# Folding two normalisation factors into one gate factor: k and v of a linear-attention layer are no longer scaled one by one

## The chip, the cores and the metric

The kernel runs on one core of a Trainium2 chip. A core has five engines that run their own instruction streams and wait for each other through semaphores: TensorE (PE in the profile, with its weight loads as PEld) for matrix products, VectorE (DVE) and GpSimd (POOL) for elementwise work on 128 partitions, ScalarE (ACT) for activation functions and copies, and SyncE (SP), which here starts transfers. The metric is the device time of one execution in microseconds (us).

## The reference, cut to what matters

The program is a network of four layers on a 256-channel image of 64 x 64 points, so on 4096 tokens of 256 features. Layers 0 and 1 are convolution-like; layer 2 is a gated linear attention and a mixture of experts; layer 3 is a softmax attention and another mixture of experts. Only the attention of layer 2 is touched. Its core is this (8 heads, 32 features a head; `L` is the token axis):

```python
q, k, v = (linear(x, w) for each of the three)           # (B, H, L, 32)
sim = einsum('bhld,bhld->bhl', q, k) * qk_norm_scale      # from the raw k
k = k / max(|k|, 1e-12)                                   # length over the 32 features of a head
v = v / max(|v|, 1e-12)
Z = einsum('bhld,bhle->bhlde', v, k) * kv_norm_scale
gates = square(relu(<Z, wg_w> + wg_b)) + 1e-5             # one number for each token and head
Z_scan = cumsum(gates * Z)                                # along the tokens
g_scan = cumsum(gates)
w = softmax-like weight from a running maximum and sum of sim
ctxt = q . (Z_scan / (g_scan + 1e-5)) * (1 + silu(w))
out = linear(ctxt, wo)
```

Everything that uses the normalised k and v uses their product Z. So the two lengths enter only as one factor r = 1/(|k||v|) for each token and head.

## The kernel before: the parts that matter

The 4096 tokens are 32 tiles of 128 (`NT`), worked on in 8 blocks (`NBLK`) of 4 tiles (`TPB`) with 512 tokens (`NB`). Inside the block the order of TensorE's instructions is the order of the calls below; the order on the other engines is chosen by a scheduler from the dependences.

```python
stages = [self.attn2_project(b, t, A, wg_bd, wp, ps) for b in range(NBLK)]
go = lambda b, *names: [stages[b][nm]() for nm in names if 0 <= b < NBLK]
with tc.manual_schedule(engines={mybir.EngineType.PE}):
    go(0, "norm", "turn")
    for b in range(-1, NBLK):
        go(b + 2, "norm")
        go(b + 1, 0)                # project tile 0 of the next block
        go(b, "lengths")
        go(b + 1, 1, 2)
        go(b, "sims")
        go(b + 1, 3)
        go(b, "turn_v")
        go(b + 2, "turn")
        go(b, "gates")
self.attn2_fac(A)                   # scans over all tokens: needs every gate and sim
```

The stages of a block (`attn2_project`, cut):

```python
room = lambda: wp.tile([P, TPB, C], F32, tag="room", name="a2_room", bufs=3)

def turn():                                                       # normalised tokens -> channels
    held["nT"] = wp.tile([P, 2, NB], F32, tag="nT", name="a2_nT", bufs=1)
    self.to_channels(ps, "a", held["n"], held["nT"], on_act=True)  # 8 PE transposes, 2 ACT copies

def project(i):
    ti, nT = b * TPB + i, held["nT"]
    for dst, lo, hi in ((A["qk"][:, ti, :], 0, 2 * C), (A["v"][:, ti, :], 2 * C, 3 * C)):
        p = ps.tile([P, hi - lo], F32, tag="b", name="a2_qkv_ps", bufs=4)
        self.mm(p, [(nT[:, kt, i * P : (i + 1) * P], w["w_qkv2"][:, kt, lo:hi]) for kt in range(2)])
        nc.vector.tensor_add(dst, p, self.row("b_qkv2")[:, lo:hi])                    # L1290

def lengths():
    ss = wp.tile([P, 2, TPB, NH], F32, tag="ss", name="a2_ss")
    for j, x in ((1, v), (0, k)):
        sq = room()
        nc.scalar.activation(sq, x, AF.Square)                                        # L1297
        nc.vector.tensor_reduce(ss[:, j], heads(sq), AX.X, ALU.add)                   # L1298
    held["tmp"] = room()
    nc.gpsimd.tensor_tensor(held["tmp"], q, k, ALU.mult)                              # L1300
    nc.vector.tensor_scalar_max(ss, ss, 1e-24)                                        # L1301
    nc.scalar.activation(ss, ss, AF.Sqrt)                                             # L1302
    nc.vector.reciprocal(ss, ss)                                                      # L1303
    nc.vector.tensor_mul(heads(v), heads(v), bc(ss[:, 1], 3, D))                      # L1304
    nc.gpsimd.tensor_tensor(heads(k), heads(k), bc(ss[:, 0], 3, D), ALU.mult)         # L1305

def sims():
    sim = wp.tile([P, TPB, NH], F32, tag="sim", name="a2_simt")
    nc.vector.tensor_reduce(sim, heads(held["tmp"]), AX.X, ALU.add)                   # L1309
    nc.vector.tensor_tensor(of("sim"), by_tile(sim), ..., ALU.mult)                   # L1310

def turn_v():
    self.to_channels(ps, "a", v, vT, on_act=True)        # 8 PE transposes, 2 ACT copies to a_vT (L226)

def gates():
    u = room()
    for i in range(0, TPB, 2):
        p = ps.tile([P, 2, 2, P], F32, tag="u", name="a2_u_ps")
        for j in range(2):
            for m in range(2):
                self.mm(p[:, j, m, :], [(vT[:, m, (i + j) * P : (i + j + 1) * P], wg_bd[:, m, :])])
        nc.vector.tensor_mul(u[:, i : i + 2, :], p..., k[:, i : i + 2, :])            # L1322
    g = wp.tile([P, TPB, NH], F32, tag="g", name="a2_g")
    nc.vector.tensor_reduce(g, heads(u), AX.X, ALU.add)                               # L1324
    nc.vector.tensor_scalar(g, g, self.row("wg_b"), 0.0, ALU.add, ALU.max)            # L1325
    nc.vector.tensor_mul(g, g, g)                                                     # L1326
    nc.vector.tensor_scalar_add(g, g, 1e-5)                                           # L1327
    nc.scalar.copy(of("gate"), by_tile(g))                                            # L1328
    nc.gpsimd.tensor_tensor(heads(k), heads(k), bc(g, 3, D), ALU.mult)                # L1329
```

The later stage (`attn2_sum`) reads v, vT and the gated k only in products of v with k.

Of the kernel before, what the change touches and what calls it, by code (L numbers as in the profile page):

```python
# [10 lines left out]
F32 = mybir.dt.float32  # L11
# [3 lines left out]
ALU = mybir.AluOpType  # L15
# [4 lines left out]
P = 128  # L20
# [6 lines left out]
TPB = NB // P  # L27
NH = 8
D = C // NH
# [51 lines left out]
def bc(ap, axis, n):  # L81

    ap = ap.unsqueeze(axis)
    shape = list(ap.shape)
    shape[axis] = n
    return ap.to_broadcast(shape)


class Net:
# [1088 lines left out]
    def attn2(self, t, S):  # L1178

        nc, tc = self.nc, self.tc  # L1180
        with tc.tile_pool(name="a2", bufs=1) as pool:
            A = {}
            A["qk"] = pool.tile([P, NT, 2 * C], F32, tag="qk", name="a2_qk")
            A["v"] = pool.tile([P, NT, C], F32, tag="v", name="a2_v")
            A["vT"] = pool.tile([P, 2, N], F32, tag="vT", name="a2_vT")

            for nm in ("sim", "gate", "fac"):
                A[nm] = pool.tile([P, 2, NT // 2, NH], F32, tag=nm, name=f"a2_{nm}")
            wg_bd = pool.tile([P, 2, P], F32, tag="wg_bd", name="wg_bd")
            self.kv_blocks(pool, None, wg_bd)  # L1190

            ked = pool.tile([P, 2, D], F32, tag="ked", name="a2_ked")
            nc.sync.dma_start(out=ked, in_=self.A["kvn_ed"].rearrange("(m p d) -> p m d", p=P, d=D))
            dif = pool.tile([P, 2, D], F32, tag="dif", name="a2_dif")
            nc.vector.tensor_tensor(dif, ked, bc(ked[:, :, 0], 2, D), ALU.not_equal)
            nc.vector.tensor_reduce(self.flags[:, 1:2], dif.rearrange("p m d -> p (m d)"), AX.X, ALU.max)
            with (
                tc.tile_pool(name="a2w", bufs=2) as wp,
                tc.tile_pool(name="a2_ps", bufs=2, space=PSUM) as ps,
            ):  # L1200
                self.rows(wp, "b_qkv2", "b_qkv2")
# [6 lines that stand above are left out]
                    for b in range(-1, NBLK):  # L1208
                        go(b + 2, "norm")
                        go(b + 1, 0)  # L1210
                        go(b, "lengths")
                        go(b + 1, 1, 2)
                        go(b, "sims")
                        go(b + 1, 3)
                        go(b, "turn_v")
                        go(b + 2, "turn")
                        go(b, "gates")
            self.attn2_fac(A)
            with (
                tc.tile_pool(name="a2x", bufs=2) as wp,  # L1220
                tc.tile_pool(name="a2x_ps", bufs=1, space=PSUM) as ps,
            ):
                bank = lambda: ps.tile([P, NB], F32, tag="r", name="f_r_ps")

                def route(t0, T):

                    n = A["qk"][:, t0 : t0 + T, :].rearrange("p t c -> p (t c)")[:, : T * CX]
                    nT = A["v"][:, t0 : t0 + T, :].rearrange("p t c -> p (t c)").rearrange("p (a n) -> p a n", a=2)
                    return self.route(t0, T, t, S, wp, n.rearrange("p (i c) -> p i c", c=CX), nT, bank)

                self.attn2_sum(t, A, ked, wp, ps, route)
            with (
                tc.tile_pool(name="a2t", bufs=1) as wp,
                tc.tile_pool(name="a2t_ps", bufs=1, space=PSUM) as ps,
            ):
                self.tile_table(S, wp, lambda: ps.tile([P, NB], F32, tag="r", name="f_r_ps"))
# [26 lines left out]

    def attn2_project(self, b, t, A, wg_bd, wp, ps):

        nc, w = self.nc, self.w
        tiles = slice(b * TPB, (b + 1) * TPB)
        pairs = slice(2 * b, 2 * b + 2)
        heads = lambda x: x.rearrange("p t (h d) -> p t h d", d=D)
        of = lambda nm: A[nm].rearrange("p a s h -> p s a h")[:, pairs]  # L1270
        by_tile = lambda x: x.rearrange("p (s a) h -> p s a h", a=2)
        q, k, v = A["qk"][:, tiles, 0:C], A["qk"][:, tiles, C:], A["v"][:, tiles, :]
        vT = A["vT"][:, :, b * NB : (b + 1) * NB]
        room = lambda: wp.tile([P, TPB, C], F32, tag="room", name="a2_room", bufs=3)
        held = {}

        def norm():
            held["n"] = wp.tile([P, TPB, C], F32, tag="n", name="a2_n", bufs=1)
            self.layer_norm(wp, t[:, tiles, :], held["n"], 1e-5, on_act=True)

        def turn():
            held["nT"] = wp.tile([P, 2, NB], F32, tag="nT", name="a2_nT", bufs=1)
            self.to_channels(ps, "a", held["n"], held["nT"], on_act=True)
# [16 lines that stand above are left out]
            nc.gpsimd.tensor_tensor(held["tmp"], q, k, ALU.mult)  # L1300
            nc.vector.tensor_scalar_max(ss, ss, 1e-24)  # L1301
            nc.scalar.activation(ss, ss, AF.Sqrt)  # L1302
            nc.vector.reciprocal(ss, ss)  # L1303
            nc.vector.tensor_mul(heads(v), heads(v), bc(ss[:, 1], 3, D))  # L1304
            nc.gpsimd.tensor_tensor(heads(k), heads(k), bc(ss[:, 0], 3, D), ALU.mult)  # L1305

        def sims():
            sim = wp.tile([P, TPB, NH], F32, tag="sim", name="a2_simt")
            nc.vector.tensor_reduce(sim, heads(held["tmp"]), AX.X, ALU.add)  # L1309
            nc.vector.tensor_tensor(of("sim"), by_tile(sim), bc(bc(self.row("qk_scale"), 1, 2), 1, 2), ALU.mult)  # L1310

        def turn_v():
            self.to_channels(ps, "a", v, vT, on_act=True)
# [8 lines that stand above are left out]
                nc.vector.tensor_mul(u[:, i : i + 2, :], p.rearrange("p t m c -> p t (m c)"), k[:, i : i + 2, :])  # L1322
            g = wp.tile([P, TPB, NH], F32, tag="g", name="a2_g")
            nc.vector.tensor_reduce(g, heads(u), AX.X, ALU.add)  # L1324
            nc.vector.tensor_scalar(g, g, self.row("wg_b"), 0.0, ALU.add, ALU.max)  # L1325
            nc.vector.tensor_mul(g, g, g)  # L1326
            nc.vector.tensor_scalar_add(g, g, 1e-5)  # L1327
            nc.scalar.copy(of("gate"), by_tile(g))  # L1328
            nc.gpsimd.tensor_tensor(heads(k), heads(k), bc(g, 3, D), ALU.mult)  # L1329

        call = lambda i: lambda: project(i)
        return {"norm": norm, "turn": turn, "lengths": lengths, "sims": sims, "turn_v": turn_v, "gates": gates,
                **{i: call(i) for i in range(TPB)}}

# [1297 lines left out]
```

## Time and profile before

The time before is 3652.96 us, the median of 3 runs (3647.47 to 3655.02). The profiled execution took 3723 us with the profiler on, a span of 3721.3 us. The table has the busy time of each engine over the whole span and over the steady part of the stage that the change touches. The stage reaches from the first projection of layer 2 (1635 us from the span's start) to the end of the last multiplication of k by its gate (1782.5 us): some 147 us or 4% of the span.

| engine | busy, whole span | share | busy, 1652 to 1780 us (128 us) |
|---|---|---|---|
| PE | 3365.0 us | 90% | 104.80 us |
| DVE | 2352.6 us | 63% | 114.30 us |
| ACT | 1413.8 us | 38% | 42.75 us |
| POOL | 1658.5 us | 45% | 58.87 us |

How to read it: the left columns say that the whole program is TensorE's; the right column says that this stage is not, at least not alone, since VectorE is the busiest engine there. No transfers of note run in the stage (1 GB/s). Lines of the profile name the engine, the source line (L1304 is the line with that comment above), the operation and the tile; "x8" is a count of instructions. TensorE's records come in pairs, two for each fp32 matrix product, and its transposes appear as `tr_ps`.

### The profile page before, as it was taken

To read this page: it belongs to the slowest core of one execution; us is meant where nothing else is said; L and a number is where in the kernel's file an instruction comes from. 1 tells how busy PE (TensorE), PEld (TensorE's weight loads), DVE (VectorE), ACT (ScalarE), POOL (GpSimd) and SP (SyncE) were. 2 spreads that over 40 slices of the span, in tenths; PEclk is the share of its full clock that TensorE was granted. 3 is DMA by queue.
4 is the path that set the end of the run, shared out by engine and by line. 5 is a ranking of instruction groups with operands and counts; after the bars stand their busy time and mean duration, and the time that the engine had idled before them with its cause. 6 is when DMAs were issued, how large, how long until landed. Compare 5 with 4: busy or idle time off the path is not lost.

```text
span 3721.3 us, 62677 instructions
## 1 busy us (share of the span) xinstructions
PE 3365.0 (90%) x23572; PEld 2388.9 (64%) x23572; DVE 2352.6 (63%) x5662; ACT 1413.8 (38%) x2891; POOL 1658.5 (45%) x1595
## 2 busy tenths in 40 slices
PE   6989999999997789888685887999999997999997
PEld 4443333333333688865564665788888886899886
DVE  6756656656565467779544547677777776555553
ACT  5544343343433566523232335322222222333332
POOL 1038888888885255634323344300000001555552
PEclk9999999999998899999786998999999998999999
DMA  1013404401012422210011865322233321555555
GB/s 57 3 28 107 137 26 124 138 24 41 21 34 94 123 63 71 72 33 1 13 36 58 261 215 217 135 90 93 95 98 97 97 91 52 219 204 209 198 192 190
DMA packets 160703, 377.44 MB, mean 101 GB/s; under 512 B 17345, under 2 KB 75458, under 8 KB 151170
## 3 DMA queue, kind: packets, MB, share of 16 engines
q1 hardware_dynamic: 136162, 317.91, 26.4%
q0 software_dynamic: 13056, 35.93, 2.5%
q10 hardware_dynamic: 11168, 19.42, 1.5%
q8 instruction: 192, 3.15, 0.4%
q14 instruction: 125, 1.02, 0.1%
HBM read 273.44 MB, written 99.76 MB: 100 GB/s over the span
## 4 chain that ended last, share of the span: by engine, by line
PE 39%; DVE 8%; issue 5%; DMA 5%; ACT 3%; POOL 3%; SPq 0%; POOLq 0%; DVEq 0%; ACTq 0%
PE a_sa_ps L2256 6%; PE f_h_ps L146 5%; PE a_oa_ps L2295 3%; PE a_ob_ps L2295 3%; PE a_oc_ps L2295 3%; DMA ys<-f_y,f_at 3%; PE a_sb_ps L2256 3%; PE f_ya_ps L146 2%; PE l_acc_ps L957 2%; PE f_yb_ps L146 2%; POOL ys L2010 1%; PE a_od_ps L2295 1%; PE a_q_ps L146 1%; PE a_sc_ps L2256 1%; PE a_s L1450 1%
## 5 line engine op out<-in xcount | busy, mean ns | idle before, releaser
L584 POOL TENSOR_TENSOR l_sm<-l_sc,mask 128x512 f32<-128x512 f32 (+3 forms) x624 | 770.7, 1272 | 119.2 <-ACT l_sc L574 116.8
L578 DVE TENSOR_TENSOR l_sm<-l_s,mask 128x256 f32<-128x256 f32 (+3 forms) x1248 | 492.3, 448 | 301.8 <-PE l_s L568 292.1
L574 ACT COPY l_sc<-l_s 128x384 f32<-128x384 f32 (+3 forms) x896 | 367.7, 461 | 558.5 <-PE l_s L568 533.5
L568 PE MATMUL l_s<-l_q,l_k 32*128 32x384 f32 (+2 forms) x3584 | 423.9, 513 | 7.4 <-ACT l_sc L574 4.1
L1826 POOL DMA_INDIRECT xs<-f_room,f_to x64 | 64.5, 1008 | 700.2 <-issue 587.2
L146 PE MATMUL f_h_ps<-f_xT,f_w 128*128 128x256 f32 x1440 | 343.2, 389 | 21.1 <-DVE f_xT L1930 8.5
L568 PEld LDWEIGHTS l_s<-l_q,l_k 32*128 32x128 f32 x3584 | 165.1, 183 | 240.7 <-issue 123.4
L146 PEld LDWEIGHTS f_h_ps<-f_xT,f_w 128*128 128x128 f32 x1440 | 262.0, 192 | 86.5 <-ACT f_h L1940 20.5
L2275 ACT ACTIVATE a_e<-a_e 128x512 f32<-128x512 f32 x256 | 155.9, 629 | 245.2 <-DVE a_e L2245 232.6
L1940 ACT ACTIVATE f_h<-f_h_ps,f_w 128x256 f32<-128x256 f32 x360 | 166.2, 470 | 169.9 <-PE f_h_ps L146 167.3
L953 DVE TENSOR_TENSOR l_pr<-l_vk,l_w_ps 128x1280 f32<-128x1280 f32 x128 | 186.6, 1482 | 54.5 <-PE l_acc_ps L957 36.2
L2010 POOL DMA_INDIRECT ys<-f_y,f_at x144 | 145.9, 1013 | 150.3 <-ACT f_y L2009 90.2
L957 PE MATMUL l_acc_ps<-ident,l_pr 128*128 128x128 f32 x1600 | 197.4, 277 | 8.2 <-POOL l_pr L948 8.1
L957 PEld LDWEIGHTS l_acc_ps<-ident,l_pr 128*128 128x128 f32 x1600 | 184.0, 143 | 14.9 <-POOL l_pr L948 9.9
L1967 POOL TENSOR_TENSOR f_wt<-f_w 128x512 f32<-128x512 f32 x72 | 90.0, 1271 | 211.5 <-PE f_ya_ps L146 198.1
L611 PE MATMUL l_a_ps<-l_sm,l_v 128*32 128x512 f32 (+3 forms) x1408 | 178.5, 528 | 2.5 <-POOL l_sm L584 2.4
L611 PE MATMUL l_b_ps<-l_sm,l_v 128*32 128x256 f32 (+2 forms) x2176 | 171.6, 376 | 0.5 <-POOL l_sm L584 0.5
L2256 PE MATMUL a_sa_ps<-a_q,a_kt 128*128 128x256 f32 x512 | 156.6, 388 | 12.7 <-DVE a_u L2261 11.6
L2260 ACT COPY a_u<-a_sa_ps 128x256 f32<-128x256 f32 x128 | 47.6, 372 | 293.6 <-PE a_sa_ps L2256 291.5
L2256 PE MATMUL a_sa_ps<-a_qt,a_kt 128*128 128x256 f32 x512 | 152.7, 380 | 0.0
L2256 PE MATMUL a_sb_ps<-a_qt,a_kt 128*128 128x256 f32 x512 | 131.4, 379 | 0.0
L2295 PE MATMUL a_ob_ps<-a_et,a_vs 128*128 128x256 f32 x512 | 131.4, 379 | 0.0
(532 smaller groups left out, 6942.1 us busy)
## 6 DMA issues: line engine op xcount, KB each, us to landing
a_kt<-a_kd SPq DMA_DIRECT2D x128, 512.0 KB
f_w<-in_f_w SPq DMA_DIRECT2D x36, 1152.0 KB
f_w<-in_f_w SPq DMA_DIRECT2D x36, 1028.0 KB
xs<-zero SPq DMA_DIRECT2D x8, 4160.0 KB
l_vk<-vt SPq DMA_DIRECT2D x180, 128.0 KB
f_x<-xs SPq DMA_DIRECT2D x72, 260.0 KB
f_w<-in_f_w SPq DMA_DIRECT2D x36, 384.0 KB
l_rcp<-l_recd SPq DMA_DIRECT2D x48, 256.0 KB
```

Of the source, the lines that this page charges most:

```text
L146: self.nc.tensor.matmul(out, lhsT, rhs, start=(i == 0), stop=(i == len(pairs) - 1))
L568: nc.tensor.matmul(s[pair, j], k[hp, key * P : (key + 1) * P], qs[hp], start=True, stop=True)
L574: nc.scalar.copy(sc[:, j], s[1, j])
L578: nc.vector.tensor_tensor(sms[0][:, j, at : at + t * wide].rearrange("p (t n) -> p t n", n=wide), part[:, which, :], mask, ALU.mult)
L584: nc.gpsimd.tensor_tensor(sms[1][:, :, at : at + t * wide].rearrange("p j (t n) -> p j t n", n=wide), part[:, :, which, :], bc(mask, 1, 2) ...
L611: nc.tensor.matmul(out, v[:, key, hp], sms[pair][:, j, base + lo * wide : base + hi * wide], start=not seen[nm], stop=(left[nm] == 0 and h ...
L953: nc.vector.tensor_tensor(pr, vk, bc(held["w"][:, j, dy], 3, D), ALU.mult)
L957: nc.tensor.matmul(acc[:, m, j, :], pf[:, dx, m * P : (m + 1) * P], self.ident, is_transpose=True, start=(j == 0 and dy == 0 and dx == 0 a ...
L1940: nc.scalar.activation(h[:, m, :], q, AF.Gelu, bias=w1[:, 2 * hidden + m : 2 * hidden + m + 1])
L2010: nc.gpsimd.indirect_dma_start(out=self.ys_parts[(i % 4) * NI + k], in_=y[:, k, :], in_offset=None, out_offset=bass.IndirectOffsetOnAxis(a ...
L2256: mm = lambda out, i, right: nc.tensor.matmul(out, A[i], right, start=True, stop=True)
L2295: nc.tensor.matmul(out, vs[:, j, i, :], right, start=(j == 0 and side != 1), stop=(j == NPAIR - 1 and side != 0))
```

## The change

Three things are changed. The factor r = 1/(|k||v|) is made once for a block (a product of the two lengths and a reciprocal of half the size), and neither v nor k is multiplied by its own factor any more: the pass over v on VectorE (L1304) and one pass over k on GpSimd (L1305) go. The gate's argument and, after the gate has been stored, the gate itself are each multiplied by r on 128 x 32 elements, so that the one remaining pass over k brings in gate and both lengths. And since v needs nothing but its projection now, its transposes move in TensorE's order from behind the next block's four projections to right behind the first of them. The purpose is to take work from the two elementwise engines and to free TensorE's transposes of v from a wait for VectorE.

```diff
@@ attn2
                         go(b + 2, "norm")
                         go(b + 1, 0)
-                        go(b, "lengths")
+                        go(b, "turn_v", "lengths")
                         go(b + 1, 1, 2)
                         go(b, "sims")
                         go(b + 1, 3)
-                        go(b, "turn_v")
                         go(b + 2, "turn")
                         go(b, "gates")
@@ attn2_project, lengths()
             nc.vector.tensor_scalar_max(ss, ss, 1e-24)
             nc.scalar.activation(ss, ss, AF.Sqrt)
-            nc.vector.reciprocal(ss, ss)
-            nc.vector.tensor_mul(heads(v), heads(v), bc(ss[:, 1], 3, D))
-            nc.gpsimd.tensor_tensor(heads(k), heads(k), bc(ss[:, 0], 3, D), ALU.mult)
+            held["r"] = wp.tile([P, TPB, NH], F32, tag="r", name="a2_r")
+            nc.vector.tensor_mul(held["r"], ss[:, 0], ss[:, 1])
+            nc.vector.reciprocal(held["r"], held["r"])
@@ attn2_project, gates()
             nc.vector.tensor_reduce(g, heads(u), AX.X, ALU.add)
+            nc.vector.tensor_mul(g, g, held["r"])
             nc.vector.tensor_scalar(g, g, self.row("wg_b"), 0.0, ALU.add, ALU.max)
             nc.vector.tensor_mul(g, g, g)
             nc.vector.tensor_scalar_add(g, g, 1e-5)
             nc.scalar.copy(of("gate"), by_tile(g))
+            nc.vector.tensor_mul(g, g, held["r"])
             nc.gpsimd.tensor_tensor(heads(k), heads(k), bc(g, 3, D), ALU.mult)
```

In the instruction streams, nothing outside this stage changes its place. Inside it, TensorE's stream differs only in the seven moved groups of transposes. The scheduler orders VectorE's steady block anew like this (t0 to t3 are the tiles of the projections that are under way): sum for sim, reciprocal of r, add of t2, `sim`, the layer norm's small steps, add of t3, the two products with u, sum for the gate, add of t0 for q and k, first gate times r, add of t0 for v, L1325's successor, the two sums of squares with the gate's steps between them, add of t1 for q and k, second gate times r, maximum of the squared lengths, add of t1 for v, product of the two lengths, and again the sum for sim.

## Prediction

> **What bounds the kernel now.** I read the windows first, since the page's shares cover 3721 us and the change touches 147 of them. Each window here runs from one block's transposes of v to the next's; the columns are length, busy time (and count) of PE, PEld, DVE, ACT, POOL, then the granted TensorE clock, the DMA share and GB/s.
>
> ```profile
> 1692.70:1709.45 16.75, 14.59 (x64) 9.37 (x65) 15.65 (x25) 6.58 (x13) 8.32 (x5) 1.00 0.00 0
> 1709.45:1726.05 16.60, 14.59 (x65) 9.37 (x65) 15.58 (x24) 6.49 (x12) 8.32 (x5) 1.00 0.00 1
> 1759.12:1771.77 12.65, 4.90 (x24) 4.21 (x25) 10.36 (x18) 3.55 (x6) 3.61 (x2) 0.70 0.00 1
> ```
>
> A steady block takes 16.6 us. DVE is busy for 15.6 of it, PE for 14.6, and no transfer runs. So DVE sets the pace, but only 2.0 us above PE. The third window is the tail behind the last projection, where PE is mostly idle.
>
> The chain of work that ended last shows the order inside a block (start, length, engine, tile, line):
>
> ```profile
> 1710.76 1.14 PE tr_ps L223 x8
> 1711.90 1.80 PE a_u_ps L146 x16
> ...
> 1716.27 1.87 DVE a_g L1325
> ...
> 1722.22 0.55 DVE a_ss L1303
> 1722.77 0.54 DVE a_qk L1290
> 1723.31 2.60 DVE a_v L1304
> 1725.91 0.14 issue
> 1726.05 0.64 PE tr_ps L223 x4
> ```
>
> It is a loop: PE's transposes of v wait for the scaling of v (L1304), the products with u come behind them, and everything from the gate's sum to L1304 is DVE again. The table of waits, taken over the stage, says how often:
>
> ```profile
> PE tr_ps L223 <- DVE a_v L1304: 17.6, 7, 7.5
> ```
>
> Seven waits, 17.6 us, the longest 7.5 us in the tail; the six others are (17.6 - 7.5) / 6 = 1.7 us each.
>
> Last the timeline of DVE and POOL, because L1304 takes 2.67 us in a steady block and 1.21 us at its fastest:
>
> ```profile
> 1722.91 1.91 POOL L1305 TENSOR_TENSOR a_qk<-a_qk,a_ss 128x1024 f32<-128x1024 f32 x1 [1.07 <-DVE a_ss L1303]
> 1723.23 2.67 DVE L1304 TENSOR_TENSOR a_v<-a_v,a_ss 128x1024 f32<-128x1024 f32 x1
> 1715.75 2.35 POOL L1300 TENSOR_TENSOR a_room<-a_qk 128x1024 f32<-128x1024 f32 x1
> 1716.18 1.95 DVE L1325 TENSOR_SCALAR a_g<-a_g,pr 128x32 f32<-128x32 f32 x1
> ```
>
> POOL's L1305 ends at 1724.82 and DVE's L1304 only 1.08 us later, about its own length: it stood still until POOL was through. L1325, on 32 elements, ends at 1718.13, just behind POOL's L1300 (1718.10); with POOL idle it took 0.24 us. So a block's DVE time holds waits for POOL: 1.46 us in L1304, some 1.65 in L1325, 0.3 in L1301.
>
> **What the Trainium skill says.** "SBUF — State Buffer", section "SBUF: two separate sides", calls the port pair that DVE and GpSimd share an exclusive lock: whoever starts first has it for the whole instruction, against a DVE operation in a 2-port mode or with two SBUF inputs. The lines above agree to 0.1 us. Its section "Who interferes with whom" adds that an operation with at most one SBUF input outside these modes doesn't contend; the reductions (1.20 us, under POOL or not) and the adds out of PSUM agree. By this the new products with r, two SBUF inputs each, can be caught as L1325 is now. "VectorE: DVE Perf Modes", section "The TRN2 errata — SBUF-src ops pay a fixed extra latency per instruction", gives (N+151)/0.96 ns for an fp32 tensor_tensor: estimates of 1224 ns for 1024 elements and 191 ns for 32. The trace has 1210 and 177 ns, and I use those. "TensorE: Matmul & The Clock Gate", section "Part 1: The HAM clock gate (the "warmup" mystery)", says an idle PE drops to half clock; the tail's 0.70 agrees.
>
> **The change, part by part.** I count DVE by steps, the distance from one start to the next, since instructions overlap by about 0.1 us.
>
> Removed from DVE in a block: the pass over v, 2.60 us, and the reciprocal of 64 elements, 0.47. Added: the reciprocal of 32 (0.55 us for 64 and 0.16 for 4 in the layer norm give 6.5 ns an element, 0.34 us, a step near 0.3) and three products of 32 elements at 0.18 us, steps of 0.1 to 0.2. POOL loses 1.91 us a block, and is no bound.
>
> The waits for POOL are what I can least read off the diff, so I walked the new order with the steps of 1709.57 to 1726.16:
> - sum for sim 1.12, reciprocal 0.3, add t2 0.93, sim 0.1, layer norm 0.4, add t3 0.93, two products with u 1.6, gate's sum 1.14, add t0 of q and k 0.6. Together 7.12.
> - First gate times r. L1300 starts as soon as the gate's sum has freed its buffer, 0.6 us earlier, and takes 2.35, so this product inherits L1325's wait: 1.85. L1325's successor then costs 0.2.
> - add t0 of v 0.33, two sums of squares with the gate's steps 2.44, add t1 of q and k 0.6, second gate times r 0.17, maximum 0.1, add t1 of v 0.4. With the line before, 13.2.
> - Product of the lengths. It starts some 0.6 us after the second gate product released POOL's pass over k (1.91 us), and has two SBUF inputs: about 1.45.
>
> The sum is 14.7 us, and 15.0 in the early blocks, which also have 0.37 us of layer-norm statistics. Of the 2.6 us of L1304, then, 1.1 was work and 1.5 was waiting, and the waiting partly comes back elsewhere.
>
> PE keeps its 14.6 us a block. Its transposes of v now come behind a projection (2.7 us), the transposes of n and the products with u, about 5.8 us after the end of the last tile's projection, while the add they need is due within 0.6 to 2.2 us. So the 1.64 and the 0.24 us waits of a block go. PE floor and DVE chain are equal within 0.4 us; I take 14.9 for the block, 1.7 less than now.
>
> Now the stage. Before, the projections of blocks 2 and 7 start at 1663.3 and 1746.7: five periods. Five at 14.9 save **9.0 us**. In the head, the first transposes of v go between earlier projections and the ACT copy between two groups falls out: **0.4 us**.
>
> The tail, from the last block's first projection: now 1746.7 to 1782.5, 35.8 us. After, PE needs 12.0 for four projections and a group of transposes, and the last v is in SBUF at about 13.8. From there DVE again: products with u of block 6 until 15.4, first sum of squares and gate's sum until 17.6, the other sum until 18.8, gate times r behind L1300 until 20.1, sum for sim until 21.3, small steps, products with u of block 7 and reciprocal until 23.7, gate's sum 24.9, gate times r behind POOL's pass of block 6 until 25.6, the gate's steps and its ACT copy until 26.7, POOL's last pass until 28.7. That is 28.8 against 35.8, **7.0 us**: the scaling of v no longer stands between the lengths and the transposes.
>
> In sum 9.0 + 0.4 + 7.0 = 16.4 us. The scans behind the stage need every gate, so what is saved here moves all that follows, and nothing else runs during the stage.
>
> **Rivals.** *All of L1304's 2.6 us leaves the loop.* If the new products slip in before POOL takes the port, DVE needs 14.7 less the 3.0 of waits and PE binds at 14.6: another 1.5 us over five blocks, and one or two in the tail; about 3634. For it: small operations often start ahead of POOL, as the tail's L1304 did (1.21 us, and POOL's L1305 stretched to 2.89). Against: L1325 is caught by L1300 in six of eight blocks.
>
> *A new wait takes the place of the old.* The second gate product also waits for ACT's copy of the gate, which stands behind the copies of vT in ACT's queue and so behind PE. The product of lengths waits for a square root on ACT. If the two add 1 us a block beyond my walk, DVE paces at some 15.9 us, and 3.5 us are left of the nine: about 3643. Against: an add of 0.4 to 0.6 us lies between each pair, ACT's small steps took 0.22 and 0.26 us, and PE has slack.
>
> *The saving disappears later.* A later stage waiting for a transfer would absorb it, leaving 3652. Against: the DMA share is 0.00 here, so no transfer spans the stage.
>
> **Range and chances.** 3652.96 - 16.4 = 3636.6, so 3637 us. The runs before spread by 7.5 us, so a median is good to some 3 us; the stage's saving I believe between 9 and 22 us. That gives 3629 to 3646. Two per cent are 73 us, half of the whole stage, so within 2% has 0.98, and either side 0.01.
>
> **What would show it.** Windows of about 14.9 us between transposes of v, with PE above 95% busy; the wait of `tr_ps` for L1304 replaced by next to nothing; the first product of gate and r near 1.9 us and the product of lengths above 1 us in the timeline, each ending with a POOL pass; the stage's end some 16 us earlier. It is wrong if periods stay above 15.5 us, if PE's transposes of v wait for the last add of v, or if the stage shortens and the end does not.

## The result, and the profile after

The changed kernel takes 3633.14 us, the median of 4 runs (3630.96 to 3635.90), against 3653.99 us before (4 runs, 3647.47 to 3655.97). That is 20.85 us less; the ratio is 0.9946, with a 95% interval from 0.9929 to 0.9964. The forecast was 3637 us, with 3629 to 3646.

The spans of profiles can't be compared across chips here: the kernel before took 3653 us on one chip and medians of 3719 to 3721 us on three others, a difference three times the size of the effect. The profiler is not the reason: the changed kernel's profiled execution took 3632.83 us, like its other runs. So times are compared only within one chip, and the profiles only by the stage. Its length, from the first projection of layer 2 to the end of the last multiplication of k by its gate, was 147.46 us (1635.04 to 1782.50) and is 125.82 us (1633.75 to 1759.57). The 21.6 us that the stage lost agree with the 20.85 us of the whole.

The windows of the changed kernel, from one block's transposes of v to the next's (columns as in the prediction: length, busy time and count of PE, PEld, DVE, ACT, POOL, clock, DMA share, GB/s):

```profile
1678.43:1693.22 14.79, 14.12 (x65) 9.44 (x64) 14.76 (x27) 6.58 (x14) 6.40 (x4) 1.00 0.00 0
1693.22:1708.02 14.80, 14.13 (x66) 9.44 (x65) 14.73 (x26) 6.58 (x14) 6.41 (x4) 1.00 0.01 1
1708.02:1722.24 14.22, 14.12 (x66) 9.44 (x64) 14.19 (x25) 6.43 (x13) 6.41 (x4) 1.00 0.00 1
1722.24:1736.19 13.95, 13.95 (x66) 9.44 (x65) 13.95 (x24) 5.01 (x9) 4.28 (x3) 1.00 0.00 1
```

Where a block took 16.6 us, it takes 14.8 in the two windows in which DVE still has small steps of the layer norm to do, and 13.9 to 14.2 behind them. Both engines are now busy nearly all the time; PE's wait for the scaling of v is gone from the table of waits, and what is left of PE's waits for DVE in the stage is this:

```profile
PE a_qkv_ps L146 <- DVE a_qk L1290: 1.3, 2, 0.7
```

The chain of work that ended last, in one of the 14.8 us blocks, no longer passes through PE at all (start, length, engine, tile, line; L1325 is now the first gate product with r, L1304 the product of the two lengths):

```profile
1694.63 1.88 DVE a_g L1325
...
1700.24 0.33 DVE a_v L1290
1700.57 1.67 DVE a_r L1304
1702.23 1.13 DVE a_simt L1309
1703.36 0.26 DVE a_r L1305
```

Both small products are as slow as the prediction feared. The timeline of DVE and POOL shows what holds the second of them:

```profile
1700.28 1.91 POOL L1331 TENSOR_TENSOR a_qk<-a_qk,a_g 128x1024 f32<-128x1024 f32 x1 [3.81 <-DVE a_ss L1301]
1700.56 1.68 DVE L1304 TENSOR_TENSOR a_r<-a_ss 128x32 f32<-128x32 f32 x1
```

GpSimd's pass over k runs until 1702.19 and the 32-element product until 1702.24. All instructions with the factor r, as a group (count, then least, median and greatest duration in ns):

```profile
L1304 DVE TENSOR_TENSOR a_r<-a_ss x8: 180/1674/1677, 1657.0 to 1753.3; 128x32 f32<-128x32 f32 x8
L1305 DVE RECIPROCAL a_r<-a_r x8: 335/337/342, 1657.7 to 1754.1; 128x32 f32<-128x32 f32 x8
L1325 DVE TENSOR_TENSOR a_g<-a_g,a_r x8: 309/1954/1977, 1664.9 to 1755.6; 128x32 f32<-128x32 f32 x8
L1330 DVE TENSOR_TENSOR a_g<-a_g,a_r x8: 174/176/191, 1670.3 to 1757.3; 128x32 f32<-128x32 f32 x8
```

The second gate product (L1330), whose pass over k only starts behind it, is never caught, that is, never held until a GpSimd pass ends.

### The profile page after: what moved, and what is told of

Same layout as the page of the kernel before. It is cut to its first block, busy times and chain, and to the rows that moved or that the text cites. A ratio compares the mean times of both kernels' runs of the same rounds, so it can differ in the third digit from the quotient of the medians.

```text
span 3631.1 us, 62669 instructions
## 1 busy us (share of the span) xinstructions
PE 3319.8 (91%) x23572; PEld 2360.4 (65%) x23572; DVE 2340.0 (64%) x5678; ACT 1413.7 (39%) x2891; POOL 1640.0 (45%) x1587
## 4 chain that ended last, share of the span: by engine, by line
PE 36%; DVE 8%; DMA 5%; issue 5%; POOL 3%; ACT 2%; SPq 0%; POOLq 0%; ACTq 0%; DVEq 0%
PE a_sa_ps L2258 5%; PE f_h_ps L146 5%; DMA ys<-f_y,f_at 3%; PE a_oa_ps L2297 3%; PE a_ob_ps L2297 3%; PE a_oc_ps L2297 3%; PE a_sb_ps L2258 2%; PE f_ya_ps L146 2%; PE f_yb_ps L146 2%; POOL ys L2012 1%; PE l_acc_ps L957 1%; PE a_od_ps L2297 1%; PE a_q_ps L146 1%; PE a_sc_ps L2258 1%; PE a_o_ps L146 1%
```

## The experiments

The head of the stage varies between profiles of one kernel: the granted clock in its first 5 us was 0.71 in one profile of the kernel before and 0.54 in another, and the first products with u came 26.4 and 27.3 us after the stage's start. So beside the stage's length I give its length from those first products with u, called the body. The steady blocks are five, each counted from its first product with u to the next block's.

| kernel | stage, us | body, us | steady blocks, us |
|---|---|---|---|
| before | 147.5 | 121.0 | 16.6 to 16.8 |
| before, second profile | 149.5 | 122.2 | 16.7 to 17.5 |
| changed | 125.8 | 99.4 | 13.9 to 14.8 |
| changed, second profile | 126.0 | 99.4 | 13.9 to 14.8 |
| fold without move | 128.8 | 103.6 | 14.9 to 15.1 |
| move without fold | 194.8 | 161.7 | 23.8 to 23.9 |
| changed, pass over v back | 131.1 | 104.7 | 15.0 to 16.2 |
| changed, pass over k back | 134.6 | 108.1 | 15.2 to 18.0 |
| before, pass over v on GpSimd | 137.1 | 112.0 | 15.4 to 15.5 |
| changed, early product | 122.1 | 97.2 | 13.9 |
| changed, early product, second profile | 123.0 | 97.2 | 13.9 |

**The kernel before, profiled again** (no edit).

> The kernel before, unchanged, for a second profile, because the first profiled execution had a span of 3721 us against 3653 us without the profiler. Measured is the stage, from the first projection of layer 2 to the end of the last multiplication of k by its gate: 147.5 us in the first profile. Expected 147.5 us again within 0.5 us, whatever the span is; if the extra 70 us lay in this stage, it would come out shorter.

The stage was 149.5 us, 2.0 us more than expected: 0.9 us in the head, and two blocks of 17.2 and 17.5 us (one of 18.2 if counted from one block's transposes of v to the next's), which the window shows with a lower clock:

```profile
1717.00:1734.30 17.30, 15.30 (x63) 10.65 (x62) 14.44 (x22) 6.58 (x12) 7.43 (x6) 0.90 0.00 0
```

So the stage's length from one profile is good to some 2 us, and the head and the clock have to be read beside it. The span was 3717.6 us and the one run took 3719.34, so this profile alone does not say whether the longer span comes from the stage. The changed kernel's two profiles do: spans of 3631.1 and 3696.6 us on two chips, with stages of 125.8 and 126.0.

**The fold without the move.**

```diff
                         go(b + 1, 0)
-                        go(b, "turn_v", "lengths")
+                        go(b, "lengths")
                         go(b + 1, 1, 2)
                         go(b, "sims")
                         go(b + 1, 3)
+                        go(b, "turn_v")
                         go(b + 2, "turn")
```

> The fold without the move: transposes of v stay behind the next block's four projections. Theory (the fold removes both VectorE's pass and what the transposes waited for; the place of the transposes adds only ACT's copy between two groups, some 0.3 us a block): stage of 127 to 130 us against 125.8 with both parts and 147.5 before, some 18 us saved in the whole. Rival (the move is what pays): stage of 140 us or more.

The stage was 128.8 us, inside the theory's range. The whole was 3704.11 us against 3720.91, a ratio of 0.9959 (0.9950 to 0.9968). The fold alone brings 121.0 - 103.6 = 17.4 us of the body's 21.6, and the move the other 4.2. A block takes 15.0 us in the mean of five against 14.3 with the move. Part of that is what was expected, PE waiting six times 0.24 us for ACT's copy between two groups of transposes. The rest was not: PE stands in the chain again, and VectorE waits 8.0 us in all for the products with u, where it is 2.1 with the move.

**The move without the fold.**

```diff
-                        go(b, "lengths")
+                        go(b, "lengths", "turn_v")
                         go(b + 1, 1, 2)
                         go(b, "sims")
                         go(b + 1, 3)
-                        go(b, "turn_v")
```

> The move without the fold: v is still scaled, and its transposes stand behind the first of the next block's projections. Theory: TensorE then waits for the lengths of the block with three projections still to do, 4 us a block or more; stage of 165 to 180 us. Rival (the early place pays by itself): stage below 147 us.

The stage took 194.8 us, longer than even the theory said, and the whole 3768.1 us in its one run. The table of waits has the reason (L1303 is here the scaling of v, L1289 the adds):

```profile
PE tr_ps L223 <- DVE a_v L1303: 56.6, 7, 8.3
DVE a_qk L1289 <- PE a_qkv_ps L146: 54.5, 24, 4.8
```

PE waits 8 us a block for the lengths, not the 4 that I gave it, and then DVE waits for the projections that stand behind the transposes. The early place is only to be had with the fold.

**A pass over v put back, with nobody waiting for it inside the loop.** It multiplies v by 1, so that only its time counts.

```diff
             nc.vector.reciprocal(held["r"], held["r"])
+            nc.vector.tensor_mul(heads(v), heads(v), bc(A["ones"], 3, D))
```

> The changed kernel with a pass over v on VectorE put back that nothing waits for but the later stage (v times 1, behind the transposes). Theory (VectorE's work sets the pace, with TensorE's floor at 13.9 us a block): blocks of 15.5 to 16.5 us, stage of 133 to 140 us. Rival (the wait of TensorE's transposes was all that cost): stage of 126 us within 1 us, blocks unchanged.

Neither was right. The stage was 131.1 us and the body 104.7, 5.3 more than without the pass; the blocks were 15.0 to 15.1 us and one 16.2. The whole, 3700.26 us against 3720.91 (0.9951, 0.9933 to 0.9970), is 20.65 us less, as if the pass cost nothing, but the interval reaches from 11 to 25 us and can't tell 5 us apart, so this rests on the body of one profile. VectorE's work does count, but less than I took: the five blocks grew by 1.25, 1.36, 0.32, 0.74 and 1.00 us, 0.93 in the mean. The pass itself ran its bare 1.21 us in the median, because here it stands where GpSimd is idle, and the product of the lengths behind it was caught for a shorter while (1.48 us in the median instead of 1.67). Why the second block grew by so much more than the third is a small step of the layer norm (L203, 0.18 us when nothing holds it): it took 1.04 and 0.18 us in these two blocks, and 0.50 and 0.79 in the same blocks of the changed kernel. With a step of 1.13 us for the pass and 0.21 less for the product, that makes some 1.5 and 0.3 us. The same pass over v had cost a step of 2.6 us in each block of the kernel before.

**A pass over k put back on GpSimd**, again a multiplication by 1.

```diff
             nc.vector.reciprocal(held["r"], held["r"])
+            nc.gpsimd.tensor_tensor(heads(k), heads(k), bc(A["ones"], 3, D), ALU.mult)
```

> The changed kernel with a pass over k on GpSimd put back (k times 1, before the products with u). Theory (GpSimd has time to spare and costs only where it holds the port that VectorE needs): up to 1.5 us a block, stage of 126 to 134 us. Rival (GpSimd's saved pass was worth nothing): 125.8 us within 0.5 us.

The stage was 134.6 us, just over the range, and the body 8.7 us longer than the changed kernel's; the one run took 3705.09 us, beside a median of 3718.88 for the kernel before. The timeline shows what a GpSimd pass can cost that no engine needs soon (L1308 is the pass, L1329 the small addition of the gate's bias, 0.23 us in the changed kernel and 1.72 in six of the eight blocks here):

```profile
1700.80 1.72 DVE L1329 TENSOR_SCALAR a_g<-a_g,pr 128x32 f32<-128x32 f32 x1
1700.58 1.91 POOL L1308 TENSOR_TENSOR a_qk<-a_qk,a_ones 128x1024 f32<-128x1024 f32 x1
```

Some 3 of the 8.7 us are one block of 18.0 us, in which PE first waited 2.17 us for DVE and then ran its next projection in 4.2 us instead of 2.85, at a lower clock (0.91 over the block).

**The kernel before with the scaling of v on GpSimd.**

```diff
-            nc.vector.tensor_mul(heads(v), heads(v), bc(ss[:, 1], 3, D))
+            nc.gpsimd.tensor_tensor(heads(v), heads(v), bc(ss[:, 1], 3, D), ALU.mult)
```

> The kernel before with the scaling of v on GpSimd instead of VectorE: VectorE loses the pass, and the transposes of v still wait for it. Theory (the loop from the lengths over the scaling to the transposes and the products with u closes through TensorE, so freeing VectorE alone gains little): blocks of 16 to 17.5 us, stage of 145 to 152 us. Rival (VectorE's work alone was the cost): blocks below 15 us, stage below 132 us.

Again between theory and rival: blocks of 15.4 to 15.5 us, a stage of 137.1, and a body 9.0 us shorter than before. The single run took 3705.66 us, beside a median of 3718.88 for the kernel before. Taking the pass from VectorE, with the transposes still waiting for it, is worth 9.0 of 21.6 us, so "gains little" was wrong. The loop is still there: PE's transposes are released by GpSimd's scaling, and PE stands between it and DVE's next products (the first line is the reciprocal of the lengths, from DVE's timeline, the others the chain):

```profile
1698.44 0.55 DVE L1303 RECIPROCAL a_ss<-a_ss 128x64 f32<-128x64 f32 x1
...
1699.08 1.92 POOL a_v L1304
1701.00 0.04 issue
1701.04 0.67 PE tr_ps L223 x4
1701.71 0.02 issue
1701.73 0.59 ACT a_vT L226
1702.33 0.04 issue
1702.37 1.15 PE tr_ps L223 x8
1703.52 1.80 PE a_u_ps L146 x16
```

It is only shorter. From the end of the reciprocal to PE's first transpose it was 3.29 us in the kernel before (1722.76 to 1726.05), with an add of 0.54 us in front of the 2.60 in which DVE waited and scaled; here GpSimd starts at once, and it is 2.05 us (1698.99 to 1701.04). These 1.24 us are about what the blocks lost (16.75 to 15.54 us), so the shorter loop alone would account for them, and the run does not separate it from a freer VectorE.

**The product of the lengths taken early.** One instruction makes the maximum and the product of the squared lengths, before one square root of half the size. The guard against a zero length of v is left out.

```diff
-            nc.vector.tensor_scalar_max(ss, ss, 1e-24)
-            nc.scalar.activation(ss, ss, AF.Sqrt)
             held["r"] = wp.tile([P, TPB, NH], F32, tag="r", name="a2_r")
-            nc.vector.tensor_mul(held["r"], ss[:, 0], ss[:, 1])
+            nc.vector.scalar_tensor_tensor(held["r"], ss[:, 0], 1e-18, ss[:, 1], ALU.max, ALU.mult)
+            nc.scalar.activation(held["r"], held["r"], AF.Sqrt)
             nc.vector.reciprocal(held["r"], held["r"])
```

> The changed kernel with the product of the two squared lengths taken before the square root, in one instruction with the maximum, which then stands right behind the second gate product (the guard against a zero length of v is left out). Theory (the product of the lengths stood still behind GpSimd's pass over k; earlier, it comes before that pass takes the port): this instruction 0.2 us instead of 1.67, the two blocks of 14.8 us down to TensorE's 13.9, stage of 123 to 124.5 us, the whole 2 us shorter. Rival (another instruction is caught instead): stage within 0.5 us of 125.8.

The five steady blocks are 13.86 us each, PE is busy in all of it, and DVE has room. The group's line and a block's window:

```profile
L1302 DVE SCALAR_TENSOR_TENSOR a_r<-a_ss x8: 175/179/186, 1655.5 to 1749.0; 128x32 f32<-128x32 f32 x8
1679.00:1692.86 13.86, 13.86 (x65) 9.52 (x64) 12.83 (x26) 6.55 (x14) 6.41 (x5) 1.00 0.01 1
```

The instruction is as large as the one it replaces, 32 elements and two SBUF inputs, and has 0.18 us in all eight blocks where that had 1.67 in the median. The other kind of instruction is not the reason, since the plain product took 0.18 to 0.19 us too in the three blocks of the changed kernel where no GpSimd pass ran beside it. It was the neighbour on GpSimd that made it long. The stage came to 122.1 us, below the range, but 1.5 us of that are the head; the body is 2.2 us shorter, as expected. The whole was 3693.74 us against 3718.88, 0.9934 (0.9921 to 0.9948).

**Both again on one chip** (no edit to either).

> The changed kernel again, beside the version with the early product on the same chip. In profiles so far, from the first products with u to the end of the stage: 99.4 us, with two blocks of 14.8 us. Expected 99.4 us within 1.5 us, and some 20 us less than the kernel before.

> The version with the early product again. From the first products with u to the end of the stage 97.2 us in its first profile, 2.2 us less than the changed kernel. Expected 97.2 us within 1 us again, all blocks at 13.9 us, and a median 1 to 4 us below the changed kernel's on this chip; if the two medians can't be told apart, the gain is only that of the stage.

The bodies repeated within 0.1 us, 99.4 and 97.2. The changed kernel took 3696.75 us (3694.63 to 3699.62) and the one with the early product 3694.68 us (3689.52 to 3696.72), against 3720.18 us before, so 23.4 and 25.5 us less: ratios of 0.9939 (0.9926 to 0.9953) and 0.9933 (0.9919 to 0.9946). The medians differ by 2.1 us and the runs overlap, so the whole does not tell the two apart by itself; the 2.2 us of the body are what is shown.

## Why the prediction was right, and where its sizes were off

The total was in the range and the direction right, and the trace has the waits and catches that were forecast. The sizes that were off were all too small and did not cancel: 9.0 + 0.4 + 7.0 = 16.4 us forecast, 11.8 + 9.8 = 21.6 in the stage with the head as it was. Point by point:

- **"PE keeps its 14.6 us a block", and the block of 14.9 us.** This is the step that was mis-sized. The early-product kernel shows PE's floor at 13.86 us, busy throughout. The 14.6 us were PE's busy time in the windows of the kernel before, and 0.73 us of them came from its stops and was no work. The projections of a block had 10.88 us as one group there (first line), a stop of 0.13 us among them, and 2.58 + 7.74 = 10.32 by steps in the changed kernel where nothing stopped them (the other two, from its chain):

```profile
1713.52 10.88 PE L146 MATMUL a_qkv_ps<-w_qkv,a_nT 128*128 128x512 f32 x32
1733.77 2.58 PE a_qkv_ps L146 x8
1737.22 7.74 PE a_qkv_ps L146 x24
```

PE stopped three times in such a block before, for 1.64, 0.24 and 0.13 us. The last instruction in front of each stop counts with 0.16 us that otherwise lie under the next one's start, 0.49 in all, and the steps behind the stops were longer by 0.24 in all. I counted DVE by steps, and should have counted PE so too. Five periods went from 83.44 to 71.62 us, 11.8 us saved instead of 9.0; with a floor of 14.6 it could not have been more than 10.4.

- **The DVE chain of 14.7, and 15.0 with statistics.** From one gate's sum to the next (starts at 1663.22, 1678.13, 1692.92 and 1707.04 in the chain) it was 14.9 us with statistics, 14.8 and 14.1 without; in the last blocks, which have fewer layer-norm steps, PE set the pace. The two new catches were read rightly: the first gate product 1.95 us in the median (a step of 1.85 was the forecast), the product of lengths 1.67 (about 1.45). A third was missed: L203, a step of the layer norm, took 0.50 and 0.79 us behind GpSimd's addition to t. The reciprocal had 0.34 us, as worked out.
- **The wait of the transposes of v goes.** So it did: PE's table of waits has no line for it. The early place of the transposes never waited for the last add of v.
- **The tail, 7.0 us.** It was 9.8: from the last block's first projection to the end it took 25.96 us where I had walked 28.8. The last v was in SBUF at 11.8 us instead of 13.8, since DVE did not trail behind PE, and the first gate product of block 6 was through at 17.5 instead of 20.1, since GpSimd's product for sim waited there for a sum of squares and not for the gate's sum, and was all but over by then.
- **The head, 0.4 us.** Some 0.8, hidden by the clock. Until the first products with u it was 26.44 us before and 26.45 after, but in the first 5 us the granted clock was 0.71 before and 0.55 after, and the next block's first projection started after 13.10 and 13.91 us. From there to the first products with u it was 13.34 us before and 12.54 after, and 13.34 and 12.56 in the second profiles.
- **"POOL loses 1.91 us a block, and is no bound".** True of the bound, but I gave the removed GpSimd pass no value apart from the wait in L1304. Putting such a pass back costs 8.7 us of the body in the place where the scheduler set it.
- **Rivals.** The first (3634 us, because the new products slip in before GpSimd) has the right total for the wrong reason: they did not slip in. The early-product kernel is near to what it describes, with PE binding, but there too the first gate product is caught (1.97 us in the median). A new wait on ACT did not show in the blocks; the only trace of one is 0.28 us in the last block. The saving did not vanish later.

What the saving is made of can be bounded, though not split cleanly. Of the body's 21.6 us, the fold brings 17.4 without the move; the move without the fold costs 40.6. Freeing VectorE of the pass, with the loop kept but shorter, brings 9.0. With the rest of the change in place, keeping a pass over v on VectorE outside the loop leaves 16.3, and keeping a pass over k on GpSimd leaves 12.9. These overlap, since each also changes which of VectorE's instructions run beside a GpSimd pass. No run takes the GpSimd pass alone out of the kernel before.

## What to carry to other kernels

When two elementwise scalings meet only in a product, one factor at the last place saves both passes and lets the matrix engine start on the raw data. A small VectorE instruction that follows the release of a large GpSimd pass should go in front of that release; its own size does not give its time (here 0.18 us in front and 1.67 behind). And before a busy share is taken for a floor, count that engine's work by steps in a stretch where nothing stops it.

## What the runs showed of the hardware that was not expected

GpSimd work off the critical path cost VectorE up to 1.8 us an instruction (the first gate product, 1.95 us in the median where the second, of the same size, had 0.18), and a pass of 1.91 us on an engine that is idle over half of the block made blocks 0.5 to 1.4 us longer, leaving aside the one at a lower clock. And TensorE's clock can dip from short waits: after a wait of 2.17 us the next projection ran in 4.2 us instead of 2.85, while a wait of 2.01 us (pass over v back) went without such a dip, and waits of 1.64 us without one in most blocks of the kernel before and with one (0.90 over a window of 17.3 us, and a block of 18.2 us from transposes to transposes instead of 16.6) in its second profile. What decides it is not shown.
